# Feature-major codes in a quantised feed-forward, and the next head stage's first keys made earlier

## The chip, the cores and the metric

The kernel runs on one core of a Trainium2 chip. The metric is device time in microseconds (us) of one execution, as the median of three runs. Five engines work side by side, each through its own queue in order: TensorE (PE, with its weight loads shown as PEld), VectorE (DVE), ScalarE (ACT), GpSimd (POOL) and SyncE (SP, which here only issues transfers). PE writes to PSUM; the other tiles lie in SBUF.

## The reference, cut to what matters

Four layers follow one another on x of 32 x 64 tokens by 128 features; each layer is an attention over a context of the same shape and then a feed-forward, both added to x. The change touches the seam between the second half of layer 2 and the first half of layer 3:

```python
# layer 2, attention: 16 heads of 8 features, causal mask, output projection
x = x + _L2_xattn_ref(_layernorm(x), ctx_1024, ctx_1024, ...)
# layer 2, feed-forward on the normed tokens, with quantised weights and activations
def quantize_a16(x):                       # ONE scale for the whole tensor
    amax = max(abs(x)); scale = 32767 / amax
    return clip(round(x * scale)) / scale
hidden = gelu(quantize_a16(x) @ W_in_q + b_in)
out = quantize_a16(hidden) @ W_out_q + b_out
x = x + out
# layer 3, attention: 16 heads of 8 features, another mask
x = x + _L3_xattn_ref(_layernorm(x), ctx_1024, ctx_1024, ...)
```

The scale of quantize_a16 is taken over all tokens. So nothing can be coded before the last group of tokens has left the attention and has been normed, and nothing of the second product can start before the last hidden value is there.

## The kernel before, in words

Tokens lie 128 to a tile, four tiles to a group (GT = 4, 512 tokens), four groups (NG = 4). K.x[g] holds a group token-major: partition = token, free axis = tile and feature. K.ctxT[g] is the context with features on the partitions.

**The order of the work.** The program is written as generators whose steps are mixed by `interleave` (L98): up to three tiles of a head stage run interleaved, and after each of their steps some steps of the tasks in K.behind are taken. The instructions come out in that program order and then pass a planner, which knows their dependencies and a cost for each and may move a later one forward on its engine where that engine would stand idle in its own reckoning. Where the author wants an order on one engine that no data forces, `in_turn` (L1344) records it as an edge without a semaphore. At run time each engine takes its queue strictly in order.

**The head stage** (`heads_xattn` L1187, with i = 0 for layer 2 and i = 1 for layer 3). For a group, `heads_inputs` norms x, turns it (PE transposes L202, ACT copy L1206) and projects queries (L1213 to L1218). `heads_keys` (L1124) makes the keys of a group: per half one product (L1131, which the profile counts as two instructions), and two ACT copies with the bias (L1141). For each tile, `heads_tile` (L1221) lets POOL spread the keys by head into the layout kb (L1233; two buffers for both head stages together), adds mask and scores on PE (L1245, L1246), takes maxima and differences on DVE (L1247, L1248), exponentials on ACT (L1249), turns them (PE L1256, ACT L1257), multiplies with the values (L1263), divides (DVE L1271, L1272), turns the group's result (L202, ACT L1286), projects it (L1291) and adds it to x (L1292). The last group ends in two halves of two tiles.

**The seam.** After each group (or half of the last) `l2_ffn_inputs` (L1374) norms x into K.l2x[g], token-major (moments L154, L155, L169 on DVE, the reciprocal root L161 on POOL, the application L183 on DVE), and takes the largest absolute value (L1382). When all groups are through, the keys of layer 3 for groups 0 and 1 are made, held behind the last product of the head stage by the chain K.l2_last. Then `l2_ffn_hidden` (L1396): one maximum over all (`global_amax`: L1315, PE L1318, L1320), the scale (L1302 to L1307), the bias row of the second product added to x on POOL for all four groups (L1401), the Gelu table (L1341). The codes (L1334: times scale plus a rounding constant; L1335: minus the constant) are taken on the token-major tiles, groups 0 and 1 as a pair, then 2 and 3, in a fixed order. For each group: four PE transposes of the codes into PSUM (L202), a bf16 high part (ACT L1419), a low part (DVE L1420), then for each of four chunks two products (L1425), Gelu on ACT (L1426) and maxima on DVE (L1429). After that come the second scale, the keys of groups 2 and 3, the Exp table and the codes of the hidden values (L1334, L1335, L1332, L1440, L1445). `l2_ffn_output` (L1451) makes the second product (L1461) and adds it to x (L1464): group 0 at once, groups 1 to 3 as tasks inside the layer-3 head stage. The first kb of layer 3 is held behind the last L1401 on POOL (L1237, L1238).

Of the kernel before, what the change touches and what calls it, by code (L numbers as in the profile page):

```python
# [1123 lines left out]
def heads_keys(K, pool, i, g, tags):  # L1124

    nc = K.nc
    kT = pool.tile([P, 2, GT, S], F32, name=f"hk{i}{g}")
    for half in range(2):
        ps = bank(K, tags[half], [P, GT, 2, S])
        w = K.wkp[i][:, half, :, :].rearrange("p r f -> p (r f)")  # L1130
        step = nc.tensor.matmul(ps.rearrange("p t b s -> p (t b s)"), w, K.ctxT[g], start=True, stop=True)  # L1131
        if i:
            in_turn(K, [K.l2_last, step])
            K.l2_last = step
        for b in range(2):
            rows = slice(b * S, (b + 1) * S)
            bias = col(K, f"{HEAD_BLOCKS[i]}_bk2", half)[rows, :]
            if i and b in KEY_DVE:
                nc.vector.tensor_scalar(kT[rows, half, :, :], ps[rows, :, b, :], bias, None, ALU.add)
            else:  # L1140
                nc.scalar.activation(kT[rows, half, :, :], ps[rows, :, b, :], AF.Identity, bias=bias)  # L1141
    K.hk[i][g] = kT
# [51 lines left out]
def heads_inputs(K, C, g):  # L1194

    nc, gp, w = K.nc, C.gp, C.w
    qn = normed(K, gp, K.x[g], "hqn")
    if (C.i, g) == (0, W3_AT):
        l3_ffn_weights(K, *K.l3w)
    if (C.i, g) == (1, 0):  # L1200
        K.l3_first = K.normed
    if C.i == 0 and g not in EARLY_CTX:
        yield from heads_context(K, K.late_v, gp, g, CTX_TAGS)
    ps = turned(K, qn, QN[C.i])
    qnT = gp.tile([P, GT, 2, S], F32, name="hqnT")
    nc.scalar.copy(qnT, ps.rearrange("p (t b s) -> p t b s", b=2, s=S))  # L1206
    yield
    ps = bank(K, QN[C.i], [P, 2, GT, S])
    hq = K.hq[g % 2]
    for b in range(2):  # L1210
        rows = slice(b * S, (b + 1) * S)
        for half in range(2):
            nc.tensor.matmul(ps[rows, half, :, :], w["Wq"][:, half * S : (half + 1) * S], qnT[:, :, b, :], start=True, stop=True)  # L1213
    scale = 1.0 / math.sqrt(8.0)
    for half in range(2):
        bias = K.hbq[:, C.i, half : half + 1]
        nc.vector.tensor_scalar(hq[0:S, half, :, 0, :], ps[0:S, half, :, :], scale, bias[0:S, :], ALU.mult, ALU.add)
        nc.scalar.activation(hq[S:P, half, :, 1, :], ps[S:P, half, :, :], AF.Identity, bias=bias[S:P, :], scale=scale)  # L1218


def heads_tile(K, C, g, t):  # L1221
# [3 lines left out]
    if t == 0:  # L1225
        C.inputs[g].finish()
        C.o = C.op.tile([P, GT, P], F32, name="ho")
    if t == AHEAD[C.i] and g + 1 < NG:
        K.behind.insert(0, C.inputs[g + 1])
    hq, o = K.hq[g % 2], C.o  # L1230
# [3 lines left out]
        kb, K.hk[C.i][g][:, :, t, :].unsqueeze(2).to_broadcast(full),  # L1234
        K.head.unsqueeze(1).unsqueeze(3).to_broadcast(full), ALU.mult,
    )
    if C.i:  # L1237
        in_turn(K, [K.l2bo_step, step])  # L1238
    yield
    nm = tp.tile([P, 16], F32, name="nm", bufs=HX_BUFS)  # L1240
    e = C.ep.tile([P, 16, S], F32, name="e")
# [132 lines left out]
def l2_ffn_inputs(K, g, tiles):  # L1374

    nc, gp = K.nc, K.l2xp
    if tiles.start == 0:
        K.l2x[g] = gp.tile([P, GT, P], F32, name=f"l2_xn{g}")
    xg, xn = K.x[g][:, tiles, :], K.l2x[g][:, tiles, :]
    ln_apply(K, xn, xg, *ln_stats(K, gp, xg))  # L1380
    at = 2 * g + tiles.start // 2
    nc.vector.tensor_reduce(K.l2am[:, at : at + 1], xn, AX.XY, ALU.max, apply_absolute_value=True)  # L1382


L2_SCALAR = (2, 3)
# [10 lines left out]
def l2_ffn_hidden(K, gp):  # L1396
    nc, wp = K.nc, K.l2p

    amax = global_amax(K, wp, K.l2am, "x")
    for xg in K.x:  # L1400
        K.l2bo_step = nc.gpsimd.tensor_tensor(xg, xg, K.l2bo.unsqueeze(1).to_broadcast([P, GT, P]), ALU.add)  # L1401
    sc, inv = scales(K, wp, amax, 1, 32767, "x")

    load_table(K, wp, AF.Gelu, sc)
# [2 lines left out]
    am = wp.tile([P, 4 * NG], F32, name="h_am")  # L1407
    nc.vector.memset(am, 0.0)
    K.l2h = []
    steps = codes(K, [K.l2x[g] for g in range(NG)], sc)  # L1410
    in_turn(K, steps)
    K.l2codes = steps[0]
    for g in range(NG):
        xn = K.l2x[g]
        ps = turned(K, xn, "t")

        hi = gp.tile([P, GN], BF16, name="xq_hi")
        lo = gp.tile([P, GN], BF16, name="xq_lo")
        nc.scalar.copy(hi, ps)  # L1419
        nc.vector.tensor_tensor(lo, ps, hi, ALU.subtract)  # L1420
        h = wp.tile([P, 4, GN], F32, name=f"l2_h{g}", tag=f"l2_h{g}")
        for c in range(4):
            ps = bank(K, ("s", "c")[c % 2], [P, GN])
# [26 lines left out]

def l2_ffn_output(K, g, tag):  # L1451
    nc, h = K.nc, K.l2h[g]
    if g in CODES_LATE:

        steps = codes(K, h, None)
        in_turn(K, [K.l3_first] + steps)
        K.l3_first = steps[-1]
# [85 lines left out]
def fused_kernel(ctx: ExitStack, tc: tile.TileContext, ins: dict, out: bass.AP):  # L1543
# [27 lines left out]
    with ExitStack() as inner:  # L1571
# [8 lines left out]
        nc.gpsimd.memset(K.l2am, 0.0)  # L1580
        K.kp = ctx.enter_context(tc.tile_pool(name="kp", bufs=KB_BUFS, side="right", reuse_waits="tile"))
        wp = ctx.enter_context(tc.tile_pool(name="l3f_w", bufs=1, side="right", reuse_waits="tile"))
        with ExitStack() as stack:
            l2_pools = heads_pools(K, stack, 0, "right")
            K.l3w = wp, stack.enter_context(tc.tile_pool(name="l3f_raw", bufs=1, reuse_waits="tile"))
# [3 lines left out]
        head_pools = heads_pools(K, inner, 1, "left")  # L1589
        with tc.tile_pool(name="l2f", bufs=2, reuse_waits="tile") as gp:  # L1590
            keys = lambda g: heads_keys(K, late_k, 1, g, KEY_TAGS)
            for g in range(KEYS_FIRST):
                keys(g)
            l2_ffn_hidden(K, gp)
            for g in range(KEYS_FIRST, NG):
                keys(g)
# [96 lines left out]
```

## Time and profile before

| what | value |
|---|---|
| median of three runs | 935.93 us (934.27 to 936.58) |
| the profiled execution's own time | 931.97 us |
| its span, first to last instruction | 930.3 us |
| mean granted TensorE clock | 0.961 |
| PE busy | 829.6 us, 89% of the span |
| DVE, ACT, POOL busy | 753.6, 558.5, 323.2 us |
| chain that ended last: PE, DVE, ACT, POOL | 56%, 25%, 12%, 2% |

The span of the profiled execution is 1.7 us shorter than its own time, and that time is 3.96 us below the median of the runs. All times within the execution are counted from its first instruction. In it the layer-2 head stage ends and the seam begins at about 737 us; the first Gelu starts at 749.96 and the last ends at 761.74; the second product starts at 765.85 and the scores of layer 3 at 784.33. In a line of the timeline the columns are start, time taken, engine, source line, operation, what is written from what, shapes and count; a line can merge several instructions of one kind, and its time is then from the first start to the last end.

### The profile page before, as it was taken

To read this page: it belongs to the slowest core of one execution; us is meant where nothing else is said; L and a number is where in the kernel's file an instruction comes from. 1 tells how busy PE (TensorE), PEld (TensorE's weight loads), DVE (VectorE), ACT (ScalarE), POOL (GpSimd) and SP (SyncE) were. 2 spreads that over 40 slices of the span, in tenths; PEclk is the share of its full clock that TensorE was granted. 3 is DMA by queue.
4 is the path that set the end of the run, shared out by engine and by line. 5 is a ranking of instruction groups with operands and counts; after the bars stand their busy time and mean duration, and the time that the engine had idled before them with its cause. 6 is when DMAs were issued, how large, how long until landed. Compare 5 with 4: busy or idle time off the path is not lost.

```text
span 930.3 us, 15748 instructions
## 1 busy us (share of the span) xinstructions
PE 829.6 (89%) x5831; PEld 677.8 (73%) x5838; DVE 753.6 (81%) x1888; ACT 558.5 (60%) x1082; POOL 323.2 (35%) x300
## 2 busy tenths in 40 slices
PE   4979999999999988899998899876999879898995
PEld 3868998989988876687786687654666537566673
DVE  5899799698689677867878778788888788779877
ACT  3545575666766598587678677542644584345432
POOL 3654564253233341401031211016344303436332
PEclk9999999999999999999999899987999999899978
DMA  8330000000000000010000000000000000000000
GB/s 186 91 91 13 1 13 12 13 1 1 12 1 1 1 13 1 14 32 1 1 1 1 1 1 2 17 7 1 1 2 1 2 0 1 2 1 1 13 13 23
DMA packets 22669, 13.73 MB, mean 15 GB/s; under 512 B 3008, under 2 KB 21952, under 8 KB 22592
## 3 DMA queue, kind: packets, MB, share of 16 engines
q1 hardware_dynamic: 18320, 10.62, 4.2%
q10 hardware_dynamic: 4272, 2.10, 0.9%
q8 instruction: 46, 0.75, 0.4%
q14 instruction: 31, 0.25, 0.1%
HBM read 11.66 MB, written 1.05 MB: 14 GB/s over the span
## 4 chain that ended last, share of the span: by engine, by line
PE 56%; DVE 25%; ACT 12%; issue 3%; DMA 2%; POOL 2%; SPq 0%; ACTq 0%; DVEq 0%; POOLq 0%
PE c_ps L916 7%; PE s_ps L1246 5%; PE g_ps L477 5%; PE s_ps L443 4%; PE c_ps L234 4%; PE g_ps L234 3%; PE g_ps L1263 3%; PE s_ps L234 3%; PE c_ps L1256 3%; PE t_ps L234 2%; PE t_ps L463 2%; ACT L934 1%; DVE hqn L183 1%; ACT L939 1%; DVE nm L445 1%
## 5 line engine op out<-in xcount | busy, mean ns | idle before, releaser
L459 POOL TENSOR_TENSOR e<-e,rs 128x512 f32<-128x512 f32 x64 | 66.0, 1041 | 97.4 <-DVE rs L458 53.0
L1233 POOL TENSOR_TENSOR kb<-hk,head 128x1024 f32<-128x1024 f32 x32 | 61.0, 1907 | 70.5 <-PE s_ps L1246 61.9
L161 POOL TENSOR_TENSOR ln_rstd<-ln_rs,neghalf 128x4 f32<-128x4 f32 (+1 forms) x38 | 39.7, 1045 | 106.9 <-DVE ln_rs L169 98.1
L443 PE MATMUL s_ps<-kvT,G 128*128 128x128 f32 x512 | 72.8, 281 | 1.0 <-DVE e L449 1.0
L443 PEld LDWEIGHTS s_ps<-kvT,G 128*128 128x128 f32 x512 | 66.8, 195 | 5.2 <-DVE e L449 1.7
L1246 PE MATMUL s_ps<-kb,hq 128*128 128x512 f32 x128 | 67.2, 608 | 0.3
L916 PE MATMUL c_ps<-mh_hi,w2e_hi 128*128 128x512 f32 x160 | 61.7, 426 | 5.0 <-ACT be L934 3.0
L477 PE MATMUL g_ps<-N,Ct 128*128 128x128 f32 x512 | 61.7, 275 | 0.0
L477 PEld LDWEIGHTS g_ps<-N,Ct 128*128 128x128 f32 x512 | 60.1, 192 | 0.8
L1247 DVE TENSOR_REDUCE nm<-s_ps 128x8 f32<-128x512 f32 x64 | 43.6, 681 | 17.5 <-PE s_ps L1246 17.1
L1257 ACT COPY hpT<-c_ps 128x512 f32<-128x512 f32 x64 | 35.3, 589 | 37.4 <-PE c_ps L1256 37.2
L467 DVE TENSOR_TENSOR pT_lo<-t_ps,pT_hi 128x512 fp32r<-128x512 f32 x64 | 43.4, 681 | 14.8 <-ACT pT_hi L466 12.5
L471 ACT COPY Ct<-c_ps 128x512 f32<-128x512 f32 x64 | 38.1, 595 | 28.6 <-PE c_ps L234 22.6
L1263 PEld LDWEIGHTS g_ps<-hv,hpT 128*64 128x64 f32 x1024 | 36.3, 144 | 23.2 <-issue 8.9
L1249 ACT ACTIVATE e<-e 128x1024 f32<-128x1024 f32 x32 | 34.0, 1061 | 31.4 <-DVE e L1248 28.6
L916 PE MATMUL c_ps<-mh_hi,w2e_lo 128*128 128x512 f32 x160 | 51.4, 401 | 0.0
L916 PE MATMUL c_ps<-mh_lo,w2e_hi 128*128 128x512 f32 x160 | 49.7, 404 | 0.7 <-DVE mh_lo L893 0.6
L450 ACT ACTIVATE e<-e 128x512 f32<-128x512 f32 x56 | 35.3, 638 | 24.7 <-DVE e L449 24.4
L893 DVE TENSOR_TENSOR mh_lo<-m,mh_hi 128x1024 fp32r<-128x1024 f32 x32 | 40.8, 1274 | 10.5 <-ACT mh_hi L892 9.7
L961 POOL TENSOR_TENSOR be<-be 128x256 f32<-128x256 f32 x16 | 16.9, 1055 | 91.3 <-DVE tg L966 90.7
L423 ACT COPY G<-g_ps 128x512 f32<-128x512 f32 x60 | 35.7, 594 | 21.5 <-PE g_ps L234 20.4
L466 ACT CAST pT_hi<-t_ps 128x512 fp32r<-128x512 f32 x64 | 37.6, 591 | 16.8 <-PE t_ps L463 10.2
(512 smaller groups left out, 2698.2 us busy)
## 6 DMA issues: line engine op xcount, KB each, us to landing
kv_tok<-in_x ACTq DMA_DIRECT2D x8, 128.0 KB, 3.5
kv_tok<-in_ctx SPq DMA_DIRECT2D x8, 128.0 KB, 2.9
x<-in_x SPq DMA_DIRECT2D x4, 256.0 KB, 8.3
ctx<-in_ctx SPq DMA_DIRECT2D x4, 256.0 KB, 3.0
w2e_raw<-in_L_ffn_expert_w SPq DMA_DIRECT2D x1, 768.0 KB, 4.4
out<-x SPq DMA_DIRECT2D x3, 256.0 KB, 2.3
WkT<-in_L_xattn_WkT ACTq DMA_DIRECT2D x2, 256.0 KB, 6.5
WqT<-in_L_xattn_WqT SPq DMA_DIRECT2D x2, 256.0 KB, 5.6
```

The costliest lines, as they stand in the source:

```text
L161: K.nc.gpsimd.tensor_tensor(out, v, K.neghalf.to_broadcast(list(v.shape)), ALU.pow)
L234: step = K.nc.tensor.matmul(ps, w[a], x[b], start=start and i == 0, stop=stop and i == 2)
L443: nc.tensor.matmul(ps[:, j, :], G[:, bb, h : h + 2, :].rearrange("p h s -> p (h s)"), kvT[:, bb, :], start=True, stop=True)
L459: nc.gpsimd.tensor_tensor(e, e, rs.unsqueeze(2).to_broadcast([P, 4, P]), ALU.mult)
L467: nc.vector.tensor_tensor(lo, ps, hi.bitcast(F32), ALU.subtract)
L477: nc.tensor.matmul(ps, Ct[:, h, :], C.N[:, h, :], start=(h == 0), stop=(h == 15))
L893: nc.vector.tensor_tensor(lo, m, hi.bitcast(F32), ALU.subtract)
L916: nc.tensor.matmul(ps, K.w2p[part][:, 2 * n + i, cols], x[:, i, :, :], start=first, stop=last)
L1233: step = nc.gpsimd.tensor_tensor(kb, K.hk[C.i][g][:, :, t, :].unsqueeze(2).to_broadcast(full), K.head.unsqueeze(1).unsqueeze(3).to_broadca ...
L1246: nc.tensor.matmul(ps, hq[:, half, t, :, :].rearrange("p b s -> p (b s)"), kb[:, half, :, :], start=False, stop=True)
L1247: nc.vector.tensor_reduce(nm[:, heads], ps, AX.X, ALU.max, negate=True)
L1263: nc.tensor.matmul(po[b * S : (b + 1) * S, j, :, :].rearrange("p r d -> p (r d)"), pT[:, j, b * S : (b + 1) * S], K.hv[g][:, 2 * t + b, C. ...
```

## The change

Five things are done.

1. `l2_ffn_inputs` norms into a passing tile (one buffer), turns it at once (four PE transposes for a group, two for a half) and copies it to SBUF on ACT. K.l2x[g] is now feature-major.
2. The codes are taken on these feature-major tiles: group 0 alone (two instructions), group 1 alone, then 2 and 3 as a pair. The transposes of L1415 are gone; the high and low parts read the codes from SBUF instead of PSUM.
3. The keys of layer 3 for group 0 are made inside the layer-2 head stage, as a task put behind when the last group's first tile begins; they are no longer in the chain K.l2_last.
4. The first kb layouts of layer 3 are no longer held behind the POOL additions L1401.
5. The addition of the bias row to x[3] leaves the seam. It is made in `l2_ffn_output` for the last group, from a copy of the row that ACT makes after it has copied the first turned queries of layer 3.

```diff
@@ heads_keys
-        if i:
+        if i and g:
             in_turn(K, [K.l2_last, step])
             K.l2_last = step
@@ heads_inputs
-    nc.scalar.copy(qnT, ps.rearrange("p (t b s) -> p t b s", b=2, s=S))
+    step = nc.scalar.copy(qnT, ps.rearrange("p (t b s) -> p t b s", b=2, s=S))
+    if (C.i, g) == (1, 0):
+        K.l3_turned = step
@@ heads_tile
+    if (C.i, g, t) == (0, NG - 1, 0):
+        K.behind.append(Task(K.first_keys()))
...
-    if C.i:
-        in_turn(K, [K.l2bo_step, step])
@@ l2_ffn_inputs
-        K.l2x[g] = gp.tile([P, GT, P], F32, name=f"l2_xn{g}")
-    xg, xn = K.x[g][:, tiles, :], K.l2x[g][:, tiles, :]
+        K.l2x[g] = gp.tile([P, GN], F32, name=f"l2_xT{g}")
+    xg = K.x[g][:, tiles, :]
+    xn = gp.tile([P, GT, P], F32, name="l2_xn")[:, tiles, :]
     ln_apply(K, xn, xg, *ln_stats(K, gp, xg))
...
+    nc.scalar.copy(K.l2x[g][:, tiles.start * P : tiles.stop * P], turned(K, xn, "t"))
@@ l2_ffn_hidden
-    for xg in K.x:
-        K.l2bo_step = nc.gpsimd.tensor_tensor(xg, xg, K.l2bo.unsqueeze(1).to_broadcast([P, GT, P]), ALU.add)
+    for xg in K.x[: NG - 1]:
+        nc.gpsimd.tensor_tensor(xg, xg, K.l2bo.unsqueeze(1).to_broadcast([P, GT, P]), ALU.add)
...
-    steps = codes(K, [K.l2x[g] for g in range(NG)], sc)
+    steps = codes(K, [K.l2x[0]], sc) + codes(K, [K.l2x[1]], sc) + codes(K, [K.l2x[g] for g in range(2, NG)], sc)
     in_turn(K, steps)
...
-        xn = K.l2x[g]
-        ps = turned(K, xn, "t")
+        xT = K.l2x[g]
...
-        nc.scalar.copy(hi, ps)
-        nc.vector.tensor_tensor(lo, ps, hi, ALU.subtract)
+        nc.scalar.copy(hi, xT)
+        nc.vector.tensor_tensor(lo, xT, hi, ALU.subtract)
@@ l2_ffn_output
+    if g == NG - 1:
+        row = K.l2p.tile([P, P], F32, name="l2_bo_late")
+        in_turn(K, [K.l3_turned, nc.scalar.copy(row, K.l2bo)])
+        nc.gpsimd.tensor_tensor(K.x[g], K.x[g], row.unsqueeze(1).to_broadcast([P, GT, P]), ALU.add)
@@ fused_kernel
+        def first_keys():
+            heads_keys(K, late_k, 1, 0, "tt")
+            yield
+
+        K.first_keys = first_keys
...
-            for g in range(KEYS_FIRST):
+            for task in K.behind:
+                task.finish()
+            K.behind.clear()
+            for g in range(1, KEYS_FIRST):
                 keys(g)
```

## The prediction

> **What bounds the kernel now.** I began with the page's first part: PE is busiest, but the average hides stages with other limits.
>
> ```profile
> PE 829.6 (89%) x5831; PEld 677.8 (73%) x5838; DVE 753.6 (81%) x1888; ACT 558.5 (60%) x1082; POOL 323.2 (35%) x300
> ```
>
> So I read the busy time by stretch for the end of the layer-2 head stage. The columns are PE, PEld, DVE, ACT and POOL busy, then the granted clock.
>
> ```profile
> 690.00:700.00 10.00, 10.00 (x103) 6.60 (x100) 8.32 (x20) 5.31 (x9) 4.20 (x4) 1.00 0.00 0
> 700.00:710.00 10.00, 9.95 (x106) 6.71 (x106) 9.09 (x25) 4.27 (x7) 5.27 (x5) 1.00 0.01 2
> 710.00:720.00 10.00, 9.41 (x98) 6.09 (x97) 7.67 (x17) 5.20 (x8) 3.65 (x3) 1.00 0.01 2
> ```
>
> PE never rests there, but for 0.6 us at 711 to 712, where DVE is late. The chain of what ended last agrees: from 680 to 730 it runs through PE almost without a break, apart from 705.0 to 712.2, where it is DVE's. Extra PE work in this stage is on the path. Extra ACT work is not, at about half busy.
>
> Next, DVE's timeline in the seam, and for comparison the same two operations on the hidden values later:
>
> ```profile
> 742.51 0.17 DVE L1307 RECIPROCAL x_inv<-x_sc 128x1 f32<-128x1 f32 x1
> 742.59 3.31 DVE L1334 TENSOR_SCALAR l_xn<-l_xn,x_sc 128x512 f32<-128x512 f32 x2
> 745.95 0.75 DVE L1335 TENSOR_SCALAR l_xn<-l_xn 128x512 f32<-128x512 f32 x2
> ...
> 764.60 0.86 DVE L1334 TENSOR_SCALAR l_h<-l_h,h_sc 128x512 f32<-128x512 f32 x2
> 765.38 0.75 DVE L1335 TENSOR_SCALAR l_h<-l_h 128x512 f32<-128x512 f32 x2
> ```
>
> Two scalings of one shape take 3.31 us at 742.59 and 0.86 at 764.60. POOL's timeline tells why: its two layouts kb fill just that time.
>
> ```profile
> 740.46 1.27 POOL L1401 TENSOR_TENSOR x<-x,l_bo 128x512 f32<-128x512 f32 x1 [0.72 <-DVE l_xn L183]
> 741.67 3.94 POOL L1233 TENSOR_TENSOR kb<-hk,head 128x1024 f32<-128x1024 f32 x2
> ```
>
> The codes end only when POOL lets go at 745.61. The same pair appears in the head stage: beside a kb at 705.73 the four applications of the norm (L183) take 2.13 us, and with POOL free 1.12.
>
> ```profile
> 706.35 2.13 DVE L183 TENSOR_SCALAR l_xn<-x,ln_mv,ln_rstd 128x128 f32<-128x128 f32 x4
> ...
> 730.79 1.12 DVE L183 TENSOR_SCALAR l_xn<-x,ln_mv,ln_rstd 128x128 f32<-128x128 f32 x4
> ```
>
> Behind the codes stand PE's transposes and then the first Gelu, from the PE and ACT timelines:
>
> ```profile
> 746.42 1.97 PE L202 MATMUL t_ps<-ident,l_xn 128*128 128x128 f32 x8 [4.00 <-DVE l_xn L1335]
> ```
> ```profile
> 747.58 0.58 ACT L1419 CAST xq_hi<-t_ps 128x512 bf16<-128x512 f32 x1 [2.65 <-PE t_ps L202]
> ...
> 749.96 0.78 ACT L1426 ACTIVATE l_h<-s_ps,cols,both_inv 128x512 f32<-128x512 f32 x1 [0.94 <-PE s_ps L1425]
> ```
>
> From 749.96 to 761.74 ACT has no gap: 16 Gelus at 0.665 from start to start and two casts at 0.47. So this part of the seam is worth what the first Gelu moves.
>
> **The head stage pays.** The keys of group 0 are four matmul instructions of 0.43 (L1131, pairs of 0.86 in the chain): 1.72 us of PE. Four transposes inline cost 0.44 (eight L1256 take 0.87): groups 0 and 1 make 0.87. Of the sum, 2.59, I let the DVE stall at 711 to 712 hide 0.6, leaving 2.0. Group 2 is normed only at 730.79 to 731.91, where the chain goes through ACT and PE by turns. Its transposes (0.44) and ACT copy (0.58, as L1206) find idle time on both (ACT 734.4 to 736.4, PE 0.5 at 735.5), and I take 0.3 for them. Group 3's transposes and its two copies (0.38 each, as L1286) fall in idle time after 737. If none of this hides, the head stage pays 3.5; if the added PE work falls mostly into stalls, 1.0. I take 2.3. DVE gets nothing new here. ACT's four key copies (4 x 0.47) and copies of groups 0 and 1 (2 x 0.58) lie beside PE.
>
> In the old place the keys of group 0 cost nothing: PE had no other work at 737 to 742, and ACT's table load ended at 744.93, before the codes.
>
> **The layouts kb.** Each needs one of two buffers, free when a scores product (L1246) of the last two tiles is done: about 723.6 and 728.25. POOL is idle from 721.84 to 729.73. I expect kb at 723.6 to 725.5 and 728.3 to 730.2. The second would hold L169 (729.49) until 730.2: 0.65 of DVE, of which the exponential at 730.83, which waits for an ACT copy anyway, sees 0.1. Bounds: 0 if both land clear, 3.8 if both fall on the last group's norm. I take 0.1, inside the 2.3, since POOL is free earlier.
>
> **The seam gains.** The steps up to x_inv stay. With POOL empty, eight codes from 742.67 take 4 x 0.39 + 4 x 0.335 (the spacing of the later rows) = 2.9; with both_inv (0.13) they end at 745.7. Group 0's codes alone end at 743.4. Before, sub and scale of group 0 ended at 746.36, then 1.1 us of transposes. Now its cast can start at 743.5, or at 743.95 if the table load (1.28 + 0.20) waits for x_sc at 742.47. The low part comes after group 0's cast; whether the queue has it ahead of the other codes the trace can't show. Bounds: ahead, Gelu starts at 743.95 + 0.60 + 0.68 + 0.38 + 0.1 = 745.7; behind all codes, at 745.7 + 0.65 + 0.38 + 0.1 = 746.85. I take the second, since in the rows of before DVE also ran all eight codes ahead of the first low part. That is 3.1 earlier. The two casts within the Gelu stretch now read SBUF: the nearest rows are ACT's casts of the context (L1164, 0.62 to the next) against 0.47, so 0.3 is lost. Gain 2.8; bounds 2.0 (should PE's clock hold the products back) and 4.0.
>
> The low part now has two SBUF inputs; the nearest row, L1165, has that too and took 0.68, as L1420 did (0.69). [...]
>
> The clock is granted at 0.50 from 745.8 to 749.2, after PE has been idle from 742.4. After the change PE is idle from about 741.8 to 744.6. It may fall again; with ACT as the limit of the next stage I take 0.
>
> **The late addition.** x[3] on POOL (1.27) moves from 740.46, where it held nobody, to about 776.5, after ACT's copy of the row (about 0.2). There it can hold the codes L1332 by 1.2 on DVE. DVE stands idle for 1.42 before 782.74, so I take 0; without that cover 1.2. Queued behind it on POOL is the reciprocal root at 780.88, which still comes in time. No DMA moves, and SP's queue gets nothing.
>
> **Sum.** 931.97 + 2.3 - 2.8 = 931.5 for an execution like the profiled one, 0.5 less. The median of the runs stood 3.96 above it, so on the median 935.93 - 0.5 = 935.4.
>
> **Rivals.**
> *Faster.* The low part goes ahead of the other codes (gain 3.95 after the casts) and the added PE work costs 1.0: 3.0 less, 932.9. For it: DVE has nothing to do for group 0 but wait. Against it: PE shows no gaps before 730 but the one.
> *Slower.* The layouts kb land on the norm of the last group (L161 at 735.75 and 739.04, L183 at 736.50 and 739.77), a chain without slack: 1.9 each, 3.8 in all, so 3.3 more, 939.2. It decides once the queue has even both of them behind 734. Against it: both buffers are free at 728.3 and POOL is idle.
> *It doesn't do what it says.* The layouts stay after the maximum and the codes are held until 745.6 all the same; only the transposes go. Group 0's second code ends at 746.0, the others near 748, the Gelu starts at 749.1: gain 0.6, cost 2.3, so 1.7 more, 937.6.
>
> **Chances.** Forecast 0.38, faster rival 0.32, slower 0.22, not done 0.08. A measurement of this kernel tells about 0.3% (2.8 us) from no change. The faster rival lies near that bound and can go beyond its price where PE's low clock later in the trace (776.5 to 779.9, 800.4 to 807.2) is missed too; I count 0.27 of its 0.32 as faster. Of the slower, 0.20, and 0.02 of the last count as slower. That leaves 0.51 for within 0.3%. The range takes in the faster rival with 2 us of such luck and the slower at its price: 931.0 to 939.2.
>
> **What would show it.** Right: L1334 in the seam at 0.4 to 0.5 each, kb before 731, first Gelu about 3 us closer to x_inv, and the stretch from 680 us to the last norm about 2.3 longer. Wrong: a kb beside the last L183; PE waiting in the head stage for a norm that POOL holds, since transposes now queue ahead of scores; or DVE late at 783 because of the late addition.

## The result, and the profile after

The changed kernel takes 938.08 us (median of 13 runs, 936.20 to 941.17). The kernel before, run again beside it, takes 932.90 us (13 runs, 928.64 to 936.58). The ratio is 1.0056, with a 95% interval of 1.0039 to 1.0072: slower by about 5.2 us. The profiled execution of the changed kernel took 939.43 us, its span is 937.7 us.

From the page of the changed kernel, PE's own line, and then the busy time by stretch of the head stage (columns PE, PEld, DVE, ACT, POOL, granted clock):

```profile
PE 836.8 (89%) x5833; PEld 679.6 (72%) x5838; DVE 751.7 (80%) x1888; ACT 562.6 (60%) x1088; POOL 324.6 (35%) x300
```
```profile
690.00:700.00 10.00, 9.39 (x82) 6.77 (x82) 10.00 (x24) 4.67 (x7) 4.32 (x3) 1.00 0.01 2
700.00:710.00 10.00, 10.00 (x76) 6.22 (x73) 7.85 (x20) 6.37 (x12) 2.29 (x2) 1.00 0.00 0
710.00:720.00 10.00, 9.93 (x107) 7.40 (x107) 7.64 (x14) 4.18 (x7) 5.67 (x3) 1.00 0.01 2
```

PE is still the busiest engine over the three rows. The first row differs from before: from 690 to 700 DVE is busy all the time and PE rests for 0.6.

The part that was forecast to gain does gain. The seam of the changed kernel, DVE's timeline and then ACT's:

```profile
753.59 0.16 DVE L1309 RECIPROCAL x_inv<-x_sc 128x1 f32<-128x1 f32 x1
753.67 0.47 DVE L1336 TENSOR_SCALAR l_xT<-l_xT,x_sc 128x512 f32<-128x512 f32 x1
...
756.17 0.69 DVE L1423 TENSOR_TENSOR xq_lo<-l_xT,xq_hi 128x512 bf16<-128x512 f32 x1
```
```profile
754.83 1.29 ACT L1422 CAST xq_hi<-l_xT 128x512 bf16<-128x512 f32 x2
...
757.83 0.78 ACT L1429 ACTIVATE l_h<-s_ps,cols,both_inv 128x512 f32<-128x512 f32 x1
```

A scaling takes 0.47 us instead of half of 3.31, and the first Gelu starts 4.07 us after x_inv ends, where it took 7.28. But x_inv comes 11.1 us later than before; 1.3 of that is there already at the end of layer 1 (620.43 against 619.09). Two places ahead of x_inv lost more than the codes won.

**The first place** is the norm of group 2. POOL, DVE and PE of the changed kernel:

```profile
730.81 1.90 POOL L1237 TENSOR_TENSOR kb<-hk,head 128x1024 f32<-128x1024 f32 x1 [0.47 <-PE s_ps L1248]
```
```profile
731.03 2.53 DVE L183 TENSOR_SCALAR l_xn<-x,ln_mv,ln_rstd 128x128 f32<-128x128 f32 x4
...
735.39 0.27 DVE L1274 TENSOR_TENSOR ho<-g_ps,rs 128x128 f32<-128x128 f32 x1
```
```profile
735.71 0.47 PE L202 MATMUL n_ps<-ident,ho 128*128 128x128 f32 x1 [1.77 <-DVE ho L1274]
736.12 1.90 PE L1265 MATMUL g_ps<-hv,hpT 128*64 128x18 f32 x32
```

The second layout kb starts when the last scores product frees its buffer, 0.2 us ahead of the norm's application, which then takes 2.53 instead of 1.12. Behind it on DVE waits the division ho, and PE, which waits for ho, stands idle for 1.77. At 735.6 the granted clock halves for 17.1 us: 32 small products (L1265) take 1.90 at 736.12, where the same number took 1.11 at 730.59.

**The second place** is PE's queue behind the last norm. DVE, then PE of the changed kernel:

```profile
748.82 0.16 DVE L1317 TENSOR_REDUCE x_one<-x_am 128x1 f32<-128x8 f32 x1
```
```profile
748.13 0.47 PE L202 MATMUL t_ps<-ident,l_xn 128*128 128x128 f32 x1 [2.25 <-DVE l_xn L183]
748.40 1.91 PE L1131 MATMUL t_ps<-ctxT,wk 128*128 128x512 f32 x2
750.11 1.91 PE L1131 MATMUL n_ps<-ctxT,wk 128*128 128x512 f32 x2
...
752.03 0.63 PE L1320 MATMUL g_ps<-ident,x_one 128*128 128x128 f32 x2
```

x_one is there at 748.98. The product that spreads it (L1320) stands in the queue behind the transposes of group 3's second half and the keys of group 1, and starts at 752.03. The two key products ahead of it take 3.4 us from start to start at half clock (748.40 to 751.81); in the kernel before two took 1.7 (737.33 to 739.05). So about half of the delay is the clock. In the kernel before, three of the four key products of groups 0 and 1 were through before x_one came, and no transpose that waits for the last norm stood ahead of them:

```profile
737.33 1.02 PE L1131 MATMUL t_ps<-ctxT,wk 128*128 128x512 f32 x2
738.19 1.02 PE L1131 MATMUL n_ps<-ctxT,wk 128*128 128x512 f32 x2
739.05 1.02 PE L1131 MATMUL t_ps<-ctxT,wk 128*128 128x512 f32 x2
741.08 0.49 PE L1318 MATMUL g_ps<-ident,x_one 128*128 128x128 f32 x2 [1.01 <-DVE x_one L1315]
```

The table gives each profiled execution by stretches, in us; e1 to e12 are the experiments of the next section. "Head" is from the last product of layer 1's feed-forward to the last scores of layer 2, "tail" from there to the start of x_one, then to the start of x_all, from the end of x_inv to the first Gelu (the 1.06 between is the same everywhere), "seam sum" is from the last product of layer 1 to the first of the second product, and "layer 3" from the first scores of layer 3 to the end of the span. Then follow the median of all runs and the ratio to the kernel before in the same set of runs.

| kernel | head | tail | to x_all | to Gelu | seam sum | layer 3 | median us | ratio (95%) |
|---|---|---|---|---|---|---|---|---|
| before | 109.16 | 12.61 | 0.74 | 7.28 | 146.76 | 145.93 | 932.90 | |
| changed | 110.23 | 18.16 | 3.88 | 4.07 | 152.87 | 147.39 | 938.08 | 1.0056 (1.0039 to 1.0072) |
| e1 layouts held | 111.04 | 13.06 | 3.88 | 4.07 | 148.55 | 145.24 | 933.57 | 0.9990 (0.9973 to 1.0006) |
| e2 maximum first | 110.23 | 18.16 | 1.05 | 4.40 | 150.37 | 149.03 | 936.18 | 1.0009 (0.9986 to 1.0032) |
| e3 both | 110.83 | 13.24 | 1.05 | 6.33 | 147.97 | 149.03 | 935.33 | 1.0009 (0.9991 to 1.0028) |
| e4 parts 1, 2 alone | 110.35 | 11.86 | 3.88 | 6.96 | 149.56 | 149.23 | 938.24 | 1.0051 (1.0029 to 1.0073) |
| e5 parts 3 to 5 alone | 110.92 | 12.93 | 0.74 | 5.04 | 146.60 | 146.10 | 933.12 | 1.0000 (0.9988 to 1.0013) |
| e6 layouts after codes | 110.80 | 13.17 | 1.05 | 4.40 | 145.93 | 145.53 | 932.39 | 0.9998 (0.9985 to 1.0011) |
| e7 filler | 110.22 | 15.59 | 3.56 | 4.50 | 150.38 | 148.63 | 937.93 | 1.0041 (1.0024 to 1.0059) |
| e8 addition in the seam | 110.24 | 18.17 | 3.88 | 4.07 | 152.87 | 145.27 | 938.04 | 1.0048 (1.0029 to 1.0066) |
| e9 before, layouts after codes | 109.09 | 12.61 | 0.74 | 5.18 | 144.57 | 146.42 | 930.96 | 0.9977 (0.9963 to 0.9990) |
| e10 layouts behind third addition | 110.29 | 13.06 | 3.13 | 4.50 | 147.48 | 145.41 | 933.20 | 1.0002 (0.9982 to 1.0022) |
| e11 e10 and maximum first | 110.25 | 13.07 | 1.05 | 4.62 | 145.50 | 145.95 | 933.39 | 1.0012 (0.9998 to 1.0026) |
| e12 as before | 109.19 | 12.61 | 0.74 | 7.34 | 146.84 | 145.97 | 932.90 | 1.0009 (0.9991 to 1.0027) |

The seam sum of the changed kernel is 6.1 us longer (152.87 - 146.76), of which 1.1 lies in the head stage, 5.55 in the tail, 3.1 before x_all, and 3.6 is won back behind x_inv (3.2 to the first Gelu, 0.4 in the stretch of the Gelus). That stands beside the 5.2 of the medians.

The seam sum leaves something out. In every kernel with part 1 the planner orders PE's queue differently from about 609 us on, ahead of the end of layer 1. From the last product that stands at the same place in all fourteen queues (it ends at 608.99 in the kernel before) to the end of layer 1 it is 10.1 without part 1 and 10.6 to 10.8 with it. So 0.5 to 0.7 us more belong to these kernels than their seam sums say.

### The profile page after: what moved, and what is told of

Read it like the earlier page. It is cut to its first block, busy times and chain, and to the rows that moved or that the text cites. A ratio compares the mean times of both kernels' runs of the same rounds, so it can differ in the third digit from the quotient of the medians.

```text
span 937.7 us, 15743 instructions
## 1 busy us (share of the span) xinstructions
PE 836.8 (89%) x5833; PEld 679.6 (72%) x5838; DVE 751.7 (80%) x1888; ACT 562.6 (60%) x1088; POOL 324.6 (35%) x300
## 3 DMA queue, kind: packets, MB, share of 16 engines
HBM read 11.66 MB, written 1.05 MB: 14 GB/s over the span
## 4 chain that ended last, share of the span: by engine, by line
PE 52%; DVE 30%; ACT 11%; issue 2%; DMA 2%; POOL 2%; SPq 0%; ACTq 0%; DVEq 0%; POOLq 0%
PE c_ps L916 6%; PE g_ps L477 5%; PE s_ps L1248 4%; PE s_ps L443 4%; PE c_ps L234 3%; PE g_ps L234 3%; PE g_ps L1265 3%; PE c_ps L1258 3%; PE s_ps L234 3%; PE t_ps L234 2%; PE t_ps L463 2%; DVE hqn L183 2%; DVE mh_lo L893 1%; DVE ln_st L154 1%; ACT L934 1%
## 5 line engine op out<-in xcount | busy, mean ns | idle before, releaser
L1265 PEld LDWEIGHTS g_ps<-hv,hpT 128*64 128x64 f32 x1024 | 37.1, 145 | 24.1 <-issue 9.6
L466 ACT CAST pT_hi<-t_ps 128x512 fp32r<-128x512 f32 x64 | 37.8, 594 | 16.7 <-PE t_ps L463 10.2
```

What stands on the lines that cost most here:

```text
L1265: nc.tensor.matmul(po[b * S : (b + 1) * S, j, :, :].rearrange("p r d -> p (r d)"), pT[:, j, b * S : (b + 1) * S], K.hv[g][:, 2 * t + b, C. ...
```

## The experiments

Three theories. **A**: the layouts kb on POOL hold DVE where they land on its norms or codes; in the changed kernel they land on group 2's norm (2.53 us instead of 1.12), PE runs dry behind it (1.77 us) and its clock halves (0.50 for 17.1 us). **B**: on PE the product for the maximum stands behind the keys of group 1. **C**: the transposes in the head stage, and the new order that comes with them, are the loss by themselves.

### e1: layouts held (parts 4 and 5 undone)

```diff
 heads_tile
+    if C.i:
+        in_turn(K, [K.l2bo_step, step])
 l2_ffn_hidden
-    for xg in K.x[: NG - 1]:
-        nc.gpsimd.tensor_tensor(xg, xg, ...)
+    for xg in K.x:
+        K.l2bo_step = nc.gpsimd.tensor_tensor(xg, xg, ...)
 l2_ffn_output: the late addition is taken out
 ...
```

> The changed kernel with parts 4 and 5 undone: the bias is added to all four groups in the seam again, and the first layouts kb of layer 3 stand behind the last addition on POOL, as before. Theory A (the layouts on POOL hold the norm of group 2, PE runs dry and its clock is halved for the whole tail): the stretch from the last scores of layer 2 to the maximum x_one goes back from 18.2 to about 13 us, with no halved clock in it before the maximum; the codes may be held by up to 3 us again; so about 3 to 4 us under the changed kernel, near 934.5. Theory B (the loss is PE's queue order: the keys of group 1 stand ahead of the product for the maximum): x_all still comes about 2 us or more after x_one, and the time hardly moves, 937 to 938. Theory C (the transposes in the head stage and the new order there are the loss): the tail stays at 17 to 18, time 938.

Measured: 933.57 beside 933.56. The norm and PE's wait behind it, from DVE's and PE's timelines of e1:

```profile
732.59 1.10 DVE L183 TENSOR_SCALAR l_xn<-x,ln_mv,ln_rstd 128x128 f32<-128x128 f32 x4
```
```profile
735.85 0.33 PE L202 MATMUL n_ps<-ident,ho 128*128 128x128 f32 x1 [1.01 <-DVE ho L1276]
```

The norm is unheld, PE's idle time is 1.01 and not 1.77, the clock stays full until 742.3, and the tail is 13.06. This carries A: with the layouts away from that norm the loss against the kernel before can no longer be told in the time. The order on PE costs its 3.1 in the trace still (x_one to x_all 3.88).

### e2: the maximum first

```diff
 global_amax
-    nc.tensor.matmul(ps, one.to_broadcast([P, P]), K.ident, ...)
+    K.max_step = nc.tensor.matmul(ps, one.to_broadcast([P, P]), K.ident, ...)
 l2_ffn_hidden
+    in_turn(K, [K.l2_last, K.max_step])
+    K.l2_last = K.max_step
+    for g in range(1, KEYS_FIRST):
+        keys(g)
 fused_kernel
-            for g in range(1, KEYS_FIRST):
-                keys(g)
 ...  (keys is handed to l2_ffn_hidden)
```

> The changed kernel with one order on PE: the product for the maximum stands ahead of the keys of group 1. Theory A: x_one to x_all falls from 3.7 to 0.6 us, but the tail before it stays at 18 us with the halved clock; 3 us under the changed kernel, near 935. Theory B: the same 3 us and that is most of the loss, 934 to 935 or lower. Theory C: 3 us at most, since the tail is what it is.

Measured: 936.18, ratio 1.0009; the interval lies below that of the changed kernel. x_one to x_all is 1.05 where it was 3.88, the tail stays at 18.16. So the order on PE is a loss of its own. Its size in the trace is 2.8; the medians show 1.9 of it (938.08 - 936.18), the ratios 4.4, so the time it is worth is not known closer than that. B as the whole loss is not what happened: the tail stays.

### e3: both edits together

The edits of e1 and of e2 in one kernel.

> Both edits together: layouts held and additions in the seam as before, and the product for the maximum ahead of the keys. Theory A: both losses go, 5 to 8 us under the changed kernel less what the codes are held, 931 to 933, so level with the kernel before or a little under it. Theory B: as e2, 934 to 935. Theory C: not under 934.

Measured: 935.33, ratio 1.0009, above the 931 to 933 that A expected and no better than e1 alone. POOL's and DVE's timelines of e3 tell where the gain went:

```profile
746.55 3.94 POOL L1237 TENSOR_TENSOR kb<-hk,head 128x1024 f32<-128x1024 f32 x2
```
```profile
747.77 0.97 DVE L1338 TENSOR_SCALAR l_xT<-l_xT,x_sc 128x512 f32<-128x512 f32 x1
748.65 1.86 DVE L1416 TENSOR_SCALAR both_inv<-wi_inv,x_inv 128x4 f32<-128x4 f32 x1
```

x_inv is there 2.4 us earlier in the execution than in e1, but the layouts, held behind the last addition on x, now lie on the codes: a scaling takes 0.97 and the tiny both_inv 1.86 (0.22 in the changed kernel). The first Gelu comes at 754.18, against 754.30 in e1. The gain turned into the next wait.

### e4: feature-major codes alone (before, with parts 1 and 2)

> The kernel before with parts 1 and 2 alone (normed tokens turned with each group, codes feature-major, group 0 first); keys of both groups, layouts and additions in the seam as before. Theory A: no layout near the norms, so the tail is about 13 us; the head stage pays under 1.5 us for the transposes; the first Gelu comes 1 to 3 us nearer to the maximum; 931 to 934. Theory B: one key pair of group 0 stands ahead of the product for the maximum, 1 to 2 us lost there, 934 to 935. Theory C: slower than before by 3 or more, 936 or over, with the loss ahead of the maximum.

Measured: 938.24, ratio 1.0051. Without the first keys in the head stage, that stage is 1.2 longer (110.35 against 109.16), x_one to x_all takes 3.88, and the layouts at 748.9 to 752.8 lie on the codes (to Gelu 6.96). So theory C holds for 1.2 us in the head stage, and the order of B comes with the transposes of parts 1 and 2 and not with the moved keys.

The time is as long as C expected (936 or over), but only 2.8 us of it lie in the seam sum. Another 3.3 of this execution lies in layer 3 (149.23 against 145.93). There the queues of e4 are not those of the kernel before: from 114.5 us behind its first scores on, 35 of PE's instructions and 85 of DVE's stand in another order. From the start of layer 3's last scores product to that of its last projection product (L1293) e4 takes 24.4 us; the kernel before, e1, e10 and e12 take 20.9. So the planner's order at the end of layer 3 is the likely cause of e4's 3.3; no run puts that order back.

### e5: keys, layouts and late addition alone (before, with parts 3 to 5)

> The kernel before with parts 3, 4 and 5 alone: first keys and layouts in the head stage, late addition; norms stay token-major, the transposes stay in the seam. Theory A: the layouts again meet the norm of group 2 on POOL; if they hold its four applications (2 us or more instead of 1.1), the tail grows by 1 to 5 us, while the codes are freed by 2.5: 932 to 936 beside 933.5. Theory B: two keys stand ahead of the maximum without a transpose in front of them, so they run early and cost nothing there: no loss from this side. Theory C (the transposes are the loss): faster than before by 2 or more.

Measured: 933.12, ratio 1.0000. From POOL's and DVE's timelines of e5:

```profile
731.44 1.90 POOL L1237 TENSOR_TENSOR kb<-hk,head 128x1024 f32<-128x1024 f32 x1 [3.55 <-PE s_ps L1248]
```
```profile
734.50 1.12 DVE L183 TENSOR_SCALAR l_xn<-x,ln_mv,ln_rstd 128x128 f32<-128x128 f32 x4
```

The early layout goes ahead of the norm's reciprocal root on POOL here. It holds the small L169 in front of that root (0.62 at 732.74, against 0.16 in e10), but it is through before the norm's application; PE waits 0.77 for ho. The tail is 12.93. What the codes win (to Gelu 5.04 instead of 7.28) the head stage pays for the keys (110.92 against 109.16). In these runs the tail is over 15 us only where a layout lies beside that application (changed, e2, e7, e8), and 11.86 to 13.24 elsewhere.

### e6: layouts after the codes (changed kernel, part 5 undone, maximum first)

```diff
 heads_tile
+    if C.i:
+        in_turn(K, [K.l2bo_step, step])
 ...  (the edits of e2, and the late addition back in the seam)
 l2_ffn_hidden, ahead of the hidden tile of a group
+        if g == NG - 1:
+            mark = wp.tile([P, 1], F32, name="l2_mark")
+            K.l2bo_step = nc.gpsimd.tensor_copy(mark, K.l2x[g][:, 0:1])
```

> The changed kernel with additions in the seam, the product for the maximum ahead of the keys, and the first two layouts held on POOL behind a copy of one element per partition of the last group's codes, so that they fall in the Gelu stretch, where no single-input DVE operation from SBUF to SBUF runs. Theory A (layouts on POOL hold DVE wherever they land on its norms or codes): neither the norms nor the codes are held, x_one to x_all 0.6, x_inv to the first Gelu about 4.0 instead of the 6.3 that the run with both edits showed: some 2 us under that run, 2 to 3 us under the kernel before, about 930.5 to 931.5 beside 933.5. Theory B or C: level with the run with both edits.

Measured: 932.39, ratio 0.9998. That is about 1 above the expected 930.5 to 931.5. The layouts start at 752.5, the codes are free, and the first Gelu comes 4.40 after x_inv. The maxima over the hidden values (L1441, reductions of SBUF tiles) run beside the layouts (752.5 to 756.3) unheld: 1.22 each from 753.29 on, as in the kernel before with POOL idle. The seam sum is 0.8 under that of before; counted from the last common product it is only 0.1 under (156.74 against 156.86). With the two places and their successor on the codes mended, the 5.2 are gone, and no gain that a measurement can tell is there.

### e9: the kernel before, with the layouts after the codes

```diff
 l2_ffn_hidden
-        K.l2bo_step = nc.gpsimd.tensor_tensor(xg, xg, ...)
+        nc.gpsimd.tensor_tensor(xg, xg, ...)
 l2_ffn_hidden, ahead of the hidden tile of a group
+        if g == NG - 1:
+            mark = wp.tile([P, 1], F32, name="l2_mark")
+            K.l2bo_step = nc.gpsimd.tensor_copy(mark, K.l2x[g][:, 0, 0:1])
```

> The kernel before with one edit: the first two layouts held behind a copy of one element per partition of the last group's codes. Theory A: the four code scalings take 0.5 us each instead of up to 2.1, the first Gelu comes 2.4 us earlier after x_inv (4.9 instead of 7.3), and the kernel gains about 2.4 us: 931 beside 933.5. If the layouts now hold the low parts or the maxima in the Gelu stretch, up to 1 to 2 us of it comes back. Theories B and C say nothing of it.

Measured: 930.96 beside 932.96, ratio 0.9977 (0.9963 to 0.9990). This is faster than the kernel before and the changed one. DVE and POOL of e9:

```profile
742.66 0.86 DVE L1334 TENSOR_SCALAR l_xn<-l_xn,x_sc 128x512 f32<-128x512 f32 x2
```
```profile
746.09 3.76 POOL L1233 TENSOR_TENSOR kb<-hk,head 128x1024 f32<-128x1024 f32 x2
```

One order on POOL gives the seam 2.1 of the 3.2 us that the change wins behind x_inv, and the head stage pays nothing. The seam sum of e6, feature-major with everything mended, is 1.4 longer (145.93 against 144.57): the codes win another 0.8 up to the first Gelu and 0.45 in the Gelu stretch (11.32 against 11.77), but the head stage costs 1.7, the tail 0.6 and x_all 0.3. The 0.7 ahead of the end of layer 1 comes on top.

### e10: layouts behind the third addition (part 4 undone only)

```diff
 heads_tile
+    if C.i:
+        in_turn(K, [K.l2bo_step, step])
 l2_ffn_hidden
     for xg in K.x[: NG - 1]:
-        nc.gpsimd.tensor_tensor(xg, xg, ...)
+        K.l2bo_step = nc.gpsimd.tensor_tensor(xg, xg, ...)
```

> The changed kernel with part 4 undone and part 5 kept: the layouts stand on POOL behind the addition to x[2], and so behind group 2's norm, but ahead of the reciprocal roots of the last group's two halves. Theory A: group 2's norm is no longer held and PE doesn't run dry at it; the second layout can delay the first root of the last group by up to 1.5 us; the tail comes to 13 to 15 us instead of 18.2, so 3 to 5 us under the changed kernel, 934 to 936 beside 933.5. Theory B: as the changed kernel, 938.

Measured: 933.20, ratio 1.0002, below the 934 to 936 that A expected. DVE and POOL of e10:

```profile
732.69 1.11 DVE L183 TENSOR_SCALAR l_xn<-x,ln_mv,ln_rstd 128x128 f32<-128x128 f32 x4
```
```profile
735.11 3.76 POOL L1237 TENSOR_TENSOR kb<-hk,head 128x1024 f32<-128x1024 f32 x2
```

The layouts take 735.1 to 738.9, between group 2's norm and the last group's, and hold neither; the tail is 13.06. This is the cleanest test of A: with part 4 alone undone the kernel stands where the one before does, and the late addition and the first keys can stay.

### e7: filler on PE

Three products of the identity by a float32 block were queued behind group 2's transposes in the changed kernel, to keep PE busy where its clock dropped.

```diff
 l2_ffn_inputs
+    if g == 2:
+        ps = bank(K, "t", [P, GN])
+        steps = [nc.tensor.matmul(ps, K.ident, K.ctxT[0], ...) for _ in range(3)]
+        in_turn(K, [K.turned_last] + steps)
```

> The changed kernel with three products of the identity by a float32 block of 512 columns (about 0.51 us each at the full clock, by L1248's 1.02 for two) queued on PE behind group 2's four transposes, where PE stood idle from 733.94 to 735.71 and its clock then halved for 17.1 us. Their results go nowhere; nothing else is changed, and kb L1237 still lies on group 2's norm (L183 still 2.5 us). If the halved clock is most of the 5.6 us that the way from the last score to x_one got longer, that way falls from 18.2 us to 13 to 15 and the kernel takes 934 to 936. If the hold of DVE by itself makes it (the norm's 1.4 us and what queues behind it), the way stays at 17 to 18 and the kernel at 938. If the clock drops at a later window of the 3.413 us grid all the same, the way falls by 1 to 2 us and the time is between.

PE's timeline of e7, and the stretch from 736 to 750 of the changed kernel and of e7:

```profile
733.50 2.74 PE L1389 MATMUL t_ps<-ctxT,ident 128*128 128x512 f32 x6
```
```profile
736.00:750.00 14.00, 11.01 (x88) 8.67 (x88) 5.76 (x24) 2.79 (x6) 1.41 (x2) 0.50 0.01 2
```
```profile
736.00:750.00 14.00, 10.08 (x94) 6.39 (x93) 6.36 (x26) 4.36 (x10) 1.40 (x2) 0.76 0.01 2
```

The products were 0.65 us too long for the gap (ho's transpose starts at 736.08; 735.43 was due, the changed kernel's 735.71 less the 0.28 by which this execution runs ahead), and the norm is held as before (2.53). The clock stays full until 742.2, and the tail falls by 2.6, to 15.59. The hold itself is 1.4 (2.53 - 1.10), and e10's tail is 13.06. The tail lies between what was expected if the clock made the loss (13 to 15) and if the hold did (17 to 18). Of the 5.1 between the changed kernel's tail and e10's, filling the gap takes back 2.6, and the longer norm application could make 1.4; about 1 is not assigned. That split is an estimate from these three executions. **The time does not confirm it**: 937.93, with an interval that overlaps the changed kernel's. In this execution layer 3 took 1.2 longer than in the changed kernel's, and how much of the clock's share is seen in most executions stays open.

### e8: the bias added in the seam (part 5 undone only)

> The changed kernel with its fifth part alone undone: the bias goes to all four groups of x in the seam, and L1459 and L1460 are gone. Theory A (the layouts on POOL at 726.6 and 730.8 hold group 2's norm) gives no change against the changed kernel, 938.1, since the way to x_one is untouched and the late addition's 1.07 us on DVE's row L1334 ended nothing. If the late addition was a cost of its own in the stage of the scores, 937.0. If the fourth addition in the seam still cost the codes their time (before: the codes ended 7.29 us before the first Gelu), 939 to 940.

Measured: 938.04, ratio 1.0048, the changed kernel's time. The late addition, on POOL from 783.95 to 785.41 in the changed kernel, does hold DVE, first in the changed kernel, then in e8:

```profile
783.35 4.35 DVE L1334 TENSOR_SCALAR l_h<-l_h 128x512 f32<-128x512 f32 x8
```
```profile
783.55 3.27 DVE L1334 TENSOR_SCALAR l_h<-l_h 128x512 f32<-128x512 f32 x8
```

The 1.08 end nothing: from the first of the second products to the scores of layer 3 it is 17.01 with the late addition and 16.89 without.

### e11: layouts behind the third addition, and the maximum first

> The changed kernel with both layouts kb behind the addition to x[2] on POOL (part 4 undone only) and the product for the maximum queued on PE ahead of the keys of group 1. By theory A with B, the layouts then lie at about 735 to 739, after group 2's norm and before the last group's, and hold neither the norm nor the codes; x_one to x_all is 1.0 us, x_inv to the first Gelu 4.1 to 4.6, so the first Gelu comes at about 751.3 where the kernel with the layouts moved alone had 754.07 and the one with layouts behind the codes 751.81. Time 931.5 to 932.5, ratio to before 0.998 to 1.000. If theory B's queue order is worth nothing by itself, the first Gelu stays at 754 and the time at 933.2. If the transposes and first keys in the head stage are the loss (theory C), it stays at 933 or above whatever the seam shows.

Measured: 933.39, ratio 1.0012 (0.9998 to 1.0026). The seam did what A and B expect, as PE's timeline of e11 shows, where x_one's product now follows x_one at once:

```profile
744.91 0.80 PE L1322 MATMUL g_ps<-ident,x_one 128*128 128x128 f32 x2 [0.18 <-DVE x_one L1319]
```

x_one to x_all is 1.05, the first Gelu comes at 751.43, and the seam sum is 2.0 under e10's. The time is not: it missed the expected 931.5 to 932.5 by about 1, and 933 or above is what C expected. From the last common product to the second product e11 is only 0.5 us shorter than the kernel before (156.33 against 156.86). From the first of the second products to the scores of layer 3 this execution took 18.47, as the kernel before did, where e10 took 16.98; the clock was at half for 3.4 us from 777.6. So C holds this far: with both places mended, the feature-major codes gain nothing that a measurement can tell.

### e12: the kernel before, with the hold moved to the third addition

```diff
-        K.l2bo_step = nc.gpsimd.tensor_tensor(xg, xg, ...)
+        step = nc.gpsimd.tensor_tensor(xg, xg, ...)
+        if xg is K.x[2]:
+            K.l2bo_step = step
```

> The kernel before with both layouts kb behind the addition to x[2] on POOL (ends 733.26) in place of the last addition. By theory A they take 733.3 to 737.1 and cover the last group's first norm (POOL's L161 at 735.75, DVE's L183 at 736.50), which moves about 1.3 us if both layouts go ahead of L161, and up to 1.9; the codes are then free (3.31 us of L1334 become about 1.7, first Gelu 5.2 after x_inv in place of 7.3). Sum 1.3 to 1.9 lost and 2.1 gained: first Gelu at 749.2 to 749.8 and 932.3 to 933.5 in time, ratio 0.998 to 1.000. If the slower rival's price holds (1.9 for each half, 3.8 in all), first Gelu at 751.7 and a time of 935. If the layouts hold nobody there, the gain is the 2.1 of the kernel with layouts behind the codes: 931.

This tests none of the three expectations: the layouts did not move, as POOL's timeline shows.

```profile
743.58 3.94 POOL L1233 TENSOR_TENSOR kb<-hk,head 128x1024 f32<-128x1024 f32 x2
```

The order of the instructions on each of the five engines is that of the kernel before: the planner left the layouts behind the last addition although nothing held them there. That makes e12 a second look at the kernel before, and a yardstick. Its median is 932.90 beside 932.74. Its profiled execution reaches the end of layer 1 at 620.97 us, 1.88 later than that of before, with one and the same queues, and its seam and layer 3 differ from those of before by 0.1 or less.

## Why the prediction was wrong

The forecast was 935.4, 0.5 us less than before and so within 0.3% of it; the kernel got slower by 0.56%.

**The step that failed** is the one on the layouts kb: "The second would hold L169 (729.49) until 730.2 ... I take 0.1". I read the time at which the buffer comes free from the trace of before (728.25) and left it there, though the same prediction moved the last scores by about 2 us. They ended at 730.66, 2.4 later (1.1 in the head stage, 1.3 already at the end of layer 1), while the norm of group 2 came at 731.03, only 0.2 later than the 730.79 of before: the layout started at 730.81, and the norm's application was held beside it. The forecast had the tail 0.3 longer for group 2's transposes; it was 5.55. e10, where part 4 alone is undone, shows that the layouts' place makes 5.1 of it (18.16 - 13.06), and its time is back at that of before. The prediction bounded this step at 3.8 by the holds alone, and for the last group. It named what would show it wrong ("PE waiting in the head stage for a norm that POOL holds"), but priced neither PE's idle time (1.77 us) nor the clock that drops behind it (0.50 for 17.1 us).

**A second step that failed**: "The steps up to x_inv stay." They did not: +3.1 from x_one to x_all. I had listed the transposes of group 3 as falling "in idle time after 737" and did not ask what they stand ahead of on PE. They wait for the last norm, so the keys queued behind them run after it, and the maximum's product after the keys. e2 takes 2.8 of it back.

**The clock**: "I take 0". It was looked for at the place where the codes wait, and it dropped 10 us earlier, at 735.6. By e7 keeping it up there is worth 2.6 us of the tail in the trace. At half clock the two keys ahead of the maximum's product also take 3.4 us from start to start, where two took 1.7 in the kernel before.

**What was right.** The codes: 3.1 earlier forecast, 3.2 measured, though by another way. The low part of group 0 went ahead of the last codes (756.17), and the table load (753.43, 1.28 us) set the first cast, so the path that the prediction had chosen was not the one taken, and the sum came out alike by luck. The late addition: 0 forecast, a hold of 1.08 on DVE and no time (e8). The low part with two SBUF inputs: 0.69, as forecast.

Two sizes were off by less. The casts from SBUF: 0.3 lost forecast, 0.4 won in the stretch of the Gelus. The prediction counted two casts there; now three of the four come ahead of the first Gelu, and the one left takes 0.51 to the next Gelu (762.49 to 763.00), where two took 0.47 each. The head stage: 2.0 forecast, 1.1 in the changed kernel and up to 1.9 in others with the same added work (e1); with the 0.7 ahead of the end of layer 1 that is 1.8 and up to 2.4.

**The rivals.** The slower one had the right mechanism (a layout on a norm that a chain waits for), put at the last group and at 3.3; it happened one group earlier, and the layouts' place cost 5.1 of the tail there, and the wait on PE's queue came on top. Neither the faster one nor the one that doesn't do what it says happened.

**The starting point.** The median 935.93 of three runs, 3.96 above the profiled execution, was high: in the sets of runs made since, the kernel before stands at 932.74 to 934.01. From 932.90 the same sum gives 932.4, so the working missed by 5.7 us and not by the 2.7 between 938.08 and 935.4. And e12 shows that two profiled executions of the same queues differ by 2 us. Of the 7.5 between the two profiled executions here, 0.65 lie ahead of the place where PE's queues part (609.64 against 608.99), and are no effect of the change.

**What stays open.** Layer 3 from its first scores took 145.2 to 149.2 us in these executions. In e4 the order of the queues there differs, and in e2, e3, e6 and e11 six of PE's products stand elsewhere; in the others PE's queue in layer 3 is that of the kernel before, and still e1 took 145.24 and e7 148.63, each with other stretches of halved clock. That is as large as most of the effects above. Whether it is why e7 and e11 gain in the seam and not in time is not shown, as each has one profiled execution. For the same reason a seam sum is not turned into a time to better than about 3 us here: e2's is 3.6 longer than that of before, its time 0.8 by the ratio. What decides which stretches are halved was not settled.

## What to carry to other kernels

When a step is let go earlier, work out its new start from the times that the rest of the change moves, and look at what stands beside it then: here a POOL operation of 1.9 us started 0.2 us ahead of a norm's application and held it (2.53 us instead of 1.12). An operation put into an in-order queue while it waits for a late result holds everything behind it (here a transpose that waited for the last norm until 748.13, and the keys behind it, put the maximum's product at 752.03, where x_one was there at 748.98), so for each one ask what follows it in that queue, not only whether the engine is idle. The fastest version moved only the two POOL layouts behind the last codes that they disturb (e9, 2.0 us faster than before), without any of the added work. And an edit can reorder queues far from where it is made, here ahead of it at 609 us and behind it in e4's layer 3, so compare the queues of the two kernels and not only the stage that was edited.

## What the runs showed of the hardware

**DVE operations with two SBUF inputs were held beside a kb too.** The prediction priced the low part by the 0.68 of L1165, without a hold, and had no row with one. In the kernel before an addition of two SBUF tiles (L1537, 128x128) takes 1.97 at 853.93, beside a kb at 853.86 to 855.76, where 0.29 is its median. The changed kernel shows it too, in DVE's and POOL's timelines:

```profile
689.07 1.91 DVE L1165 TENSOR_TENSOR ctx_lo<-ctxT,ctx_hi 128x512 fp32r<-128x512 f32 x1
```
```profile
686.68 3.76 POOL L1237 TENSOR_TENSOR kb<-hk,head 128x1024 f32<-128x1024 f32 x2 [4.60 <-PE t_ps L234]
```

L1165 took 0.68 where POOL was free (694.69), and here it ends 0.5 us after POOL lets go at 690.44. A small operation was held as well: both_inv, 128x4, took 1.86 in e3, beside the layouts at 746.55 to 750.49, and 0.22 in the changed kernel. Reductions of an SBUF tile were not: a maximum of e9 (L1432, 128x1024) took 1.22 at 749.40, beside a kb that ends at 749.85, and those of e6 1.22 each beside the layouts; in the kernel before, with POOL idle, it is 1.22.

**The granted clock dropped on a grid.** In the kernel before, the stretches at half clock from 622.9 us on start at 622.9, 745.8, 776.5, 800.4, 858.4, 895.9, 916.4 and 926.7. These starts lie 36, 9, 7, 17, 11, 6 and 3 steps of 3.413 us apart, and the first of the execution, at 69.9, lies 251 such steps ahead of the last. There and in the changed kernel the stretches last 3.4 us or a multiple of it (6.8, 10.2, 17.1), but for the last one, which the end of the execution cuts. In the changed kernel an idle stretch of 1.77 us was followed by 17.1 us at half clock, although PE was busy for 11.0 of the 14 us from 736 on; one of 1.01 us, in e1 and e10, was not followed by a drop there (32 products L1267 take 1.11 behind it). Idle time alone did not decide here: in the kernel before the clock drops at 895.9, although PE was busy for 3.18 of the 3.41 us before it, twelve of its 21 products there being only 8 columns wide.
